# Finer score tables, more gathers and expert units beside the last attention, and a third of the tail's products on GpSimd

## The chip, the cores and the metric

The kernel runs on one NeuronCore of one Trainium2 chip, in one launch. The metric is the device time of that core in microseconds (us), the median of three runs. The engines are named as in the profile: PE (TensorE), DVE (VectorE), ACT (ScalarE), POOL (GpSimd) and SP (SyncE, which issues most DMAs).

## The reference, cut to what matters

A float32 tensor of 4 batch entries, 32 x 96 tokens and 256 channels goes through two layers. Layer 0 is a group norm and two state-space passes (along one axis, then the other). Layer 1 is an additive attention inside each batch entry, and then a graph network over all 12,288 tokens that decides how four expert networks are mixed:

```python
# attention, for each of 4 batch entries, 3072 tokens, U = 32
h = tanh(q[:, :, None, :] + k[:, None, :, :] + bh)      # q, k: 32 numbers a token
a = softmax(einsum('biju,u->bij', h, Wa) + ba)          # 3072 x 3072 scores
t = t + einsum('bij,bjd->bid', a, ln(t))

# graph: 1,048,576 edges, indices up to 65,536 (out-of-range ones clamp or are dropped)
h = (x_flat @ W_gat).reshape(M, HEADS, NUM_EXPERTS)     # 4 x 4 features a token
a_src, a_dst = (h * att_src).sum(-1), (h * att_dst).sum(-1)
e = leaky_relu(a_src[src] + a_dst[dst])
alpha = softmax of e over the edges into the same dst
agg = segment_sum(h[src] * alpha, dst)                  # 16 numbers a token
scores = layernorm(agg).reshape(M, HEADS, NUM_EXPERTS).mean(1)
w, idx = softmax(top_2(scores))
for ei in range(4):                                     # experts, 256 -> 512 -> 256
    hh = gelu(x @ W1[ei] + b1[ei])
    out += g[ei] * (hh @ W2[ei] + b2[ei])
```

The experts themselves don't need the graph; only their weights g do. The graph needs the features of every source and destination token, so it needs the attention's output.

## The kernel before, in words

The tokens lie in 96 tiles of 128 rows (24 tiles, `NT`, to a batch entry; 12, `T8`, to a half entry, of which there are 8, `N8`). The order of the work on PE, ACT, DVE and POOL is the order in which the Python program emits it: nothing is reordered, each engine runs its own list, and a wait holds everything behind it on that engine. What is interleaved, and how densely, is set by small budgets in microseconds that the program counts down while it is built. They are constants of the program, not measurements.

**The stages.** Until about 11.1 ms, Layer 0 and the attentions of entries 0 to 2 run together. Then the attention of entry 3 runs with other work beside it until 13.57 ms. A short drain follows, and then the tail: the graph and the rest of the experts.

**The last attention** (`Attention.units`). The attention goes in slots. Each has one tanh of 128 x 3072 on ACT (L1047), and eight matmuls of 384 columns on PE that turn an earlier tanh into scores (L1020, `scores`). Three tanh buffers lie between ACT and PE. After eight slots the 32 rows of one unit are complete: DVE takes the maximum (L1108), ACT the exponential (L1115), PE transposes (L1124) and multiplies with the values (L1133). After four units (32 slots) a tile is put together. For that POOL makes four small factors `sf` (L1192), on which PE waits (L1197). An entry has 768 slots and 96 units.

In each slot, `steps` in `whole` may add four kinds of work beside the attention:
- DVE sorts the edge list (`Edges.sort`) and, once it is sorted (`ed.listed`), makes one-hot tables of edges in bfloat16 (L1500), which PE multiplies into a count (`products`, L1514, eight matmuls, counted at 8 x `PRODUCT_US`).
- PE computes expert units ahead (`Experts.early`). A unit is 512 tokens through one expert: eight matmuls of 512 columns, sixteen of 256. Units go in pairs, and the two Gelus of a pair (L1965) come together on ACT.
- The two above draw on the same PE budget, `us_t`, which grows by `SLOT_US` a slot, less what the attention's own steps take. At most one set of products is taken in a slot; expert matmuls take what is left.
- POOL issues one or two gathers a slot (`columns`, L1276). A gather is an indirect DMA that fetches one row of a score table for each of 128 edges. `gather` reads destination scores from `tab_a`, `early` reads source rows from `tab_e`. The list `columns` has 360 of the first (half entries 0 to 5) and 216 of the second. It is begun when the tables of entries 0 to 2 are written. In each of these slots `pace` puts a copy of one element of the current tanh on POOL (L901), so that POOL can't run ahead of ACT.

`tab_a` is a DRAM tensor for each batch entry: a gather from one waits for all of its 24 tiles. The tables of entry 3 are written by `after` in four pieces while its attention still runs, the last of them behind it.

**The tail** (`tail`). A planner walks over half steps, six to an expert unit, with its own clock: 2.7 us a half step (`HALF_US`), 2.0 us more for each group of one-hot products (`GROUP_US`), 1.6 us for a gather that is still wanted (`GATHER_US`). What was gathered beside the attention is in `ed.have`, and only the rest is wanted. For each of 8 half entries there are five jobs of 12 edge columns. A job has scores, values, and three groups of four columns (`u0` = 0, 4, 8). For a group, `spread` makes on DVE a one-hot of lanes `ol`, a one-hot of tiles `oh` (L1663), and the product of `oh` with the features, `rh` (L1667, 128 x 960). A half step later `place` adds them up on PE in four matmuls of 240 columns (L1677). With all 120 groups planned, the expert units run on alone. When a quarter's groups are done, `finish` computes its gates on DVE, and then the kept expert outputs are weighted and summed there (L2006). The gathers of a half step come behind a `pace` of the tail: POOL copies a mark (L1612) that DVE writes (L1611), so POOL can't run ahead of DVE.

The lists `wanted`, `jobs` and `calls` are plain Python, so the interleaving of the tail follows from the counts alone.

Of the kernel before, what the change touches and what calls it, by code (L numbers as in the profile page):

```python
# [17 lines left out]
F32 = mybir.dt.float32  # L18
# [4 lines left out]
ALU = mybir.AluOpType  # L23
# [3 lines left out]
P = 128  # L27
B, NV, S, C = 4, 32, 96, 256
TOK = NV * S
M = B * TOK  # L30
NT = TOK // P
# [15 lines left out]
CT = 2  # L47
# [3 lines left out]
HEADS, NEXP, FF = 4, 4, 512  # L51
# [5 lines left out]
W1, W2, C1 = EW // 4, 512, 464  # L57
C2, CL, CY = 384, 112, 280
N8, T8, CE, LATE = 8, 12, 60, 24
EARLY = 4, 5, 0, 1, 6, 7  # L60
G1, K1 = 8, 4
GP, GG = 12, 4
EDGE_US = 2.3
# [1 line left out]
GATHER_US, HALF_US, GROUP_US, LAND_US = 1.6, 2.7, 2.0, 10.0  # L65
QUARTERS = 2, 0, 3, 1
KO_BUFS = 2
SLOT_US, PRODUCT_US = 1.2, 0.11
EU, EG = 32, 2
TB = 512  # L70
NQ, FC, NBLK_X = TB // P, FF // P, M // TB
# [2 lines left out]
ROW = HEADS + HF  # L74
# [777 lines left out]
class Attention:  # L852
# [4 lines left out]
    def __init__(self, ctx, tc, ident, a, x1, x2, xn2T, tab_s, tab_a, keys, l0):  # L857
        self.nc = nc = tc.nc
        self.ident, self.x1, self.x2, self.xn2T = ident, x1, x2, xn2T
        self.tab_s, self.tab_e, self.tab_a = *tab_s, tab_a  # L860
        pool = lambda name, bufs, **k: ctx.enter_context(
            tc.tile_pool(name=name, bufs=bufs, side="right", **k))
        const = self.const = pool("atc", 1)
        self.rows, self.th, self.wk = pool("atr", 2), pool("atb", TH_BUFS), pool("atw", 1)
        self.ps_e = pool("ate", PE_BUFS, space=PSUM)
        self.ps_v = pool("atv", PV_BUFS, space=PSUM)

        def load(name, shape, ap):
            t = const.tile(shape, F32, tag=name, name=name)
            nc.sync.dma_start(t, ap)  # L870
            return t

        self.l0, self.kq, self.krep, self.qsel = l0, keys, keys.krep, keys.qsel
        self.wa = load("wa_blk", [P, P // (4 * R_ATT), QU], a["wa_blk"])
        self.ba = load("ba_rep", [P, 1], a["ba_rep"])
        self.wg = load("wg", [P, KC, HF], a["W_gat"].rearrange("(k p) f -> p k f", p=P))
        self.asr = load("as_rep", [P, HF], a["as_rep"])
        self.adr = load("ad_rep", [P, HF], a["ad_rep"])
        self.eps = const.tile([P, 1], F32, tag="eps1", name="eps1")
        nc.vector.memset(self.eps, 1e-5)  # L880

        self.sel = const.tile([P, QU], F32, tag="sel", name="sel")
        nc.vector.tensor_tensor(self.sel, ident[:, :QU], ident[:, QU:2 * QU], ALU.add)
        for q in range(2, P // QU):
            nc.vector.tensor_tensor(self.sel, self.sel, ident[:, q * QU:(q + 1) * QU], ALU.add)
        self.state = [{} for _ in range(B)]

        self.extra, self.entry, self.col, self.asked, self.normed = 0.0, 0, 0, 0, 0
        self.now, self.reduces, self.more, self.tc = None, False, [], tc
        self.mark = const.tile([P, 1], F32, tag="mark", name="mark")  # L890

        self.later = []
# [318 lines left out]
    def after(self, b, t0=0, t1=NT):  # L1211

        nc, mv = self.nc, self.state[b]["mv2"]
        j0, N = t0 // CT, t1 // CT
        x2 = self.x2[b * TOK:(b + 1) * TOK, :]
        x = self.tiles_of(x2, j0)
        rs = self.inverse_roots(mv, t0, t1)
        yield
        for j in range(j0, N):
            rowsd = slice(b * TOK + j * CT * P, b * TOK + (j + 1) * CT * P)  # L1220
            ahead = self.tiles_of(x2, j + 1) if j + 1 < N else None
            for i in range(CT):
                self.normalized(x[:, i, :], x[:, i, :], mv, rs, j * CT + i)
            yield
            xT = self.transposed(x)
            nc.sync.dma_start(self.xn2T[:, :, rowsd].rearrange("k p m -> p k m"), xT)
            x = ahead
            yield
            ph = self.psum("ph")
            for i in range(CT):  # L1230
                for k in range(KC):
                    nc.tensor.matmul(ph[:, i * HF:(i + 1) * HF], xT[:, k, i * P:(i + 1) * P],
                                     self.wg[:, k, :], start=(k == 0), stop=(k == KC - 1))
            hb = self.wk.tile([P, CT, ROW], F32, tag="hb", name="hb")
            db = self.wk.tile([P, CT, HEADS], F32, tag="db", name="db")
            nc.vector.tensor_copy(hb[:, :, HEADS:],
                                  ph[:, :CT * HF].rearrange("p (n f) -> p n f", f=HF))
            tmp = self.wk.tile([P, CT, HF], F32, tag="gtmp", name="gtmp")
            for rep, dst in ((self.asr, hb), (self.adr, db)):
                nc.vector.tensor_tensor(tmp, hb[:, :, HEADS:],  # L1240
                                        rep.unsqueeze(1).to_broadcast([P, CT, HF]), ALU.mult)
                nc.vector.tensor_reduce(dst[:, :, 0:HEADS],
                                        tmp.rearrange("p n (h x) -> p n h x", x=NEXP),
                                        AX.X, ALU.add)
            n0 = b * NT + j * CT
            nc.sync.dma_start(self.tab_s[:, n0:n0 + CT, :], hb)
            if b < B - 1:
                nc.sync.dma_start(self.tab_e[:, n0:n0 + CT, :], hb)
            nc.sync.dma_start(self.tab_a[b][:, j * CT:(j + 1) * CT, :], db)
            if j == NT // CT - 1:  # L1250
                self.normed = b + 1
            yield


class Edges:
# [23 lines left out]

    def gather(self, k, c):  # L1280
        self.have.add((k, c, "d"))
        self.indirect(self.gd[:, k, c, :], self.tab_a[k // 2], self.di[:, k, c:c + 1])

    def early(self, k, c):
        self.have.add((k, c, "s"))
# [2 lines left out]
    def columns(self):  # L1288

        first = [(self.gather, k, c) for k in range(N8 - 2) for c in range(CE)]  # L1290
        return first + [(self.early, k, c) for k in EARLY for c in range(LATE, CE)]

    @staticmethod
    def halves(t):
# [58 lines left out]
    def sort(self):  # L1353


        nc, v, tc = self.nc, self.nc.vector, self.tc
        v.tensor_scalar(self.tiles, self.lanes[:, :NH], float(P), None, ALU.add)
        with ExitStack() as ctx:
# [4 lines left out]
            with tc.tile_pool(name="es", bufs=1) as lists:  # L1363
# [42 lines left out]
                c = w["keep"]  # L1406
# [10 lines left out]
                there, last = float((B - 1) * TOK + VALID), w["keep"][:, :C2]  # L1417
# [10 lines left out]
                part, tl = w["keep"][:, :W], w["keep"][:, W:2 * W]  # L1428
# [10 lines left out]
                n = N8 * CE  # L1439
# [11 lines left out]
                for of, rows in ((s3, self.si), (x3, self.di)):  # L1451
                    v.tensor_scalar(d, of, VALID - 1, None, ALU.bitwise_and)
                    v.tensor_scalar(lo, d, P - 1, None, ALU.bitwise_and)
                    v.tensor_scalar(hi, d, 7, None, ALU.logical_shift_right)
                    if rows is self.di:
                        v.tensor_scalar(lo, lo, float(NT), None, ALU.mult)
                        for q in range(1, B):
                            part = hi[:, 2 * q * CE:2 * (q + 1) * CE]
                            v.tensor_scalar(part, part, float(-q * NT), 0.0, ALU.add, ALU.max)
                    else:  # L1460
                        late, soon = split(lo)[:, :, :LATE], split(lo)[:, :, LATE:]
                        v.tensor_scalar(late, late, float(NH), None, ALU.mult)
                        v.tensor_scalar(soon, soon, float(NH - NT), None, ALU.mult)
                        tile = split(hi)[:, :, LATE:]
                        v.tensor_scalar(tile, tile, float(NH - NT - 1), None, ALU.min)
                    v.tensor_tensor(flat(rows), lo, hi, ALU.add)
                    yield 1.8
# [58 lines left out]
class Graph:  # L1526
# [35 lines left out]
    def tables(self):  # L1562
# [2 lines left out]
        self.hall = hall = new("hall", [P, NH, ROW])  # L1565
        adst = self.adst = new("adst", [P, NH, 2 * HEADS])
        nc.sync.dma_start(hall, self.tab_s)
        for q in range(4):
            nc.sync.dma_start(adst[:, q * NT:(q + 1) * NT, 0:HEADS], self.tab_a[q])
        last = self.last = new("last", [P, ROW])  # L1570
        nc.sync.dma_start(last, self.tab_s[P - 1, NH - 1, :].unsqueeze(0).to_broadcast([P, ROW]))

# [80 lines left out]
    def spread(self, k, g, u0):  # L1653
# [6 lines left out]
        for to, among, which in ((ol, ed.lanes, ed.lane),  # L1660
# [3 lines left out]
                                    which[:, k, cols].unsqueeze(2).to_broadcast([P, GG, n]),  # L1664
                                    ALU.is_equal)
        v = self.v[k, g][:, u0:u0 + GG, :]
        nc.vector.tensor_tensor(rh, oh.unsqueeze(3).to_broadcast([P, GG, T8, ROW]),  # L1667
                                v.unsqueeze(2).to_broadcast([P, GG, T8, ROW]), ALU.mult)
        return ol, rh

# [564 lines left out]
def whole(tc, a, dram, out):  # L2235
# [8 lines left out]

    tab_s = dram.tile([P, NH, ROW], F32, tag="tab_s", name="tab_s")
    tab_e = dram.tile([P, NH - NT, ROW], F32, tag="tab_e", name="tab_e")
    tab_a = [dram.tile([P, NT, HEADS], F32, tag=f"tab_a{b}", name=f"tab_a{b}") for b in range(B)]
    with ExitStack() as ctx:
        actx, lctx, ectx = ExitStack(), ExitStack(), ExitStack()
        with tc.manual_schedule(engines={E.PE, E.Activation, E.DVE, E.Pool}):  # L2250
# [8 lines left out]
            def steps():  # L2259
# [22 lines left out]
                while True:  # L2282
# [10 lines left out]
                    if columns:  # L2293
                        att.pace()
                        turn = 3 - turn
                        for f, k, c in columns[:turn]:
                            f(k, c)
                        del columns[:turn]
                    us_t = min(us_t, SLOT_US) + SLOT_US - att.extra
                    if ed.todo and us_t > 0:  # L2300
                        ed.todo.pop(0)()
                        us_t -= G1 * PRODUCT_US
# [108 lines left out]
```

## Time and profile before

| | us |
|---|---|
| median of 3 runs | 14503.21 (14501.98 to 14504.32) |
| the profiled execution | 14508.64 |
| its span, first to last instruction | 14506.8 |
| ACT busy | 12278.6 (85%) |
| PE busy | 11322.4 (78%) |
| DVE busy | 10473.8 (72%) |
| POOL busy | 9080.5 (63%) |

The busy shares are averages over stages that have different limits, so they say little by themselves. The two stages that the change touches are the last attention and the tail. Busy time of the four engines in five stretches, and the granted share of PE's clock:

| from, to (us) | what | PE | DVE | ACT | POOL | clock |
|---|---|---|---|---|---|---|
| 12100 to 13569 | last attention with gathers and products | 1312.8 of 1469 | 496.6 | 1436.2 | 690.5 | 0.97 |
| 13569 to 13640 | drain | 52.9 of 71 | 16.5 | 9.2 | 1.4 | 0.93 |
| 13640 to 13970 | tail, groups dense | 272.8 of 330 | 222.6 | 105.9 | 243.5 | 0.93 |
| 13970 to 14320 | tail, groups as gathers land | 300.8 of 350 | 250.6 | 86.4 | 232.3 | 0.94 |
| 14320 to 14507 | tail, expert units alone | 177.4 of 187 | 101.1 | 38.5 | 0.4 | 0.98 |

A busy PE is not a PE at its peak: matmuls are pipelined, and their ends are modelled. A gather's busy time on POOL is that of issuing it. The chain that ended last is empty in this profile, so the bounds have to be read from the stages and from the waits.

### The profile page before, as it was taken

The numbers are of one execution on the slowest core, as the hardware profiler recorded it, in microseconds if no ns is written. First come the engines' busy times: TensorE is split into PE (matmuls) and PEld (weight loads), VectorE is DVE, ScalarE is ACT, GpSimd is POOL, SyncE is SP. The second block draws the span as 40 slices with busy tenths as digits, with TensorE's granted clock in tenths as the row PEclk, the third lists the DMA queues.
The fourth block names the chain that finished last, engine by engine and source line by source line (L and its number), as shares of the span: only waits on it lengthen the run. The fifth ranks groups of instructions, "written<-read, shape, count | busy, mean of one in ns | idle before, by whom it ended". The sixth has DMA issues, their size and how long they took to land.

```text
span 14506.8 us, 224766 instructions
## 1 busy us (share of the span) xinstructions
PE 11322.4 (78%) x86704; PEld 5143.5 (35%) x86704; DVE 10473.8 (72%) x15217; ACT 12278.6 (85%) x9676; POOL 9080.5 (63%) x7108
## 2 busy tenths in 40 slices
PE   5777767777777777778887677788887788888888
PEld 2333322222232333333333233333333334443566
DVE  7888987787777877777777777757776785332376
ACT  4555569999999899999998899999999999999522
POOL 5777777777777667767776677747764003653373
PEclk8989978888888889989998899999989999999999
DMA  6778864445545444455554444435543100110233
GB/s 216 237 236 241 248 188 148 148 150 153 150 151 153 148 148 154 150 149 157 156 154 146 148 149 152 156 107 152 155 151 110 39 22 17 12 18 15 61 102 125
DMA packets 1199839, 1984.19 MB, mean 137 GB/s; under 512 B 418596, under 2 KB 646436, under 8 KB 1193636
## 3 DMA queue, kind: packets, MB, share of 16 engines
q1 hardware_dynamic: 1168036, 1963.77, 44.1%
q0 software_dynamic: 30720, 5.96, 0.9%
q8 instruction: 682, 11.17, 0.3%
q14 instruction: 401, 3.28, 0.1%
HBM read 1859.14 MB, written 110.18 MB: 136 GB/s over the span
## 4 chain that ended last, share of the span: by engine, by line


## 5 line engine op out<-in xcount | busy, mean ns | idle before, releaser
L1047 ACT ACTIVATE th<-krep,qsel 128x3072 f32<-128x3072 f32 x3072 | 8658.0, 2850 | 284.4 <-PE pe L1020 273.8
L1020 PE MATMUL pe<-th,wa_blk 128*32 128x384 f32 x49152 | 4933.7, 529 | 932.2 <-ACT pr L1115 691.0
L515 POOL TENSOR_TENSOR h<-h,bC 128x768 f32<-128x768 f32 x2048 | 3765.3, 1840 | 2769.4 <-DVE h L508 2198.2
L508 DVE TENSOR_TENSOR_SCAN h<-dA,dB 128x384 f32<-128x384 f32 x3008 | 2706.5, 941 | 895.9 <-ACT dA L470 673.8
L1020 PEld LDWEIGHTS pe<-th,wa_blk 128*32 128x32 f32 x49152 | 1468.5, 115 | 3408.8 <-issue 1877.1
L483 DVE TENSOR_TENSOR dB<-bB,dtu 128x768 f32<-128x768 f32 x1912 | 1809.9, 947 | 97.0 <-DMA bB<-bc 45.9
L522 POOL TENSOR_TENSOR h<-h 128x768 f32<-128x768 f32 x752 | 1413.5, 1880 | 53.6
L1133 PE MATMUL pv<-xn,pT 128*32 128x257 f32 x18432 | 1156.6, 401 | 216.7 <-DVE pT L1126 215.4
L470 ACT ACTIVATE dA<-dt,t_A 128x380 f32<-128x380 f32 x2048 | 1121.2, 571 | 230.2 <-DVE h L508 162.6
L534 PE MATMUL py<-h,ident 128*128 128x384 f32 x2176 | 930.0, 558 | 478.5 <-POOL h L515 370.4
L470 ACT ACTIVATE dA<-dt,d_A 128x372 f32<-128x372 f32 x2048 | 1107.2, 564 | 139.3 <-DVE h L508 91.8
L503 DVE TENSOR_TENSOR_SCAN h<-dA,dB 128x768 f32<-128x768 f32 x544 | 947.7, 1751 | 127.3 <-ACT dA L470 81.3
L1192 POOL TENSOR_SCALAR sf<-sel,f 128x32 f32<-128x32 f32 x384 | 137.3, 384 | 1239.3 <-ACT f L1188 1238.8
L1133 PEld LDWEIGHTS pv<-xn,pT 128*32 128x32 f32 x18432 | 598.4, 115 | 851.1 <-DVE pT L1126 373.7
L1108 DVE TENSOR_REDUCE nb<-pe 128x1 f32<-128x768 f32 x384 | 364.2, 948 | 729.0 <-PE pe L1020 697.1
L523 POOL TENSOR_TENSOR h<-h 128x384 f32<-128x384 f32 x752 | 790.4, 1051 | 59.0
L524 POOL TENSOR_TENSOR y<-y,h 128x384 f32<-128x384 f32 x752 | 777.1, 1033 | 59.0
L534 PEld LDWEIGHTS py<-h,ident 128*128 128x128 f32 x2176 | 420.2, 209 | 941.0 <-POOL h L515 583.5
L1124 PE MATMUL ptw<-ident,pr 128*128 128x128 f32 x2304 | 459.2, 314 | 306.4 <-DVE pT L1126 128.1
L1126 DVE COPY pT<-ptw 128x512 f32<-128x512 f32 (+1 forms) x768 | 417.6, 544 | 327.3 <-PE ptw L1124 315.4
L1276 POOL DMA_INDIRECT gd<-tab_a,di x480 | 498.3, 1038 | 159.2 <-issue 156.7
L1124 PEld LDWEIGHTS ptw<-ident,pr 128*128 128x128 f32 x2304 | 295.7, 159 | 770.9 <-issue 281.3
(329 smaller groups left out, 15071.9 us busy)
## 6 DMA issues: line engine op xcount, KB each, us to landing
bB<-bc SPq DMA_DIRECT2D x2048, 384.0 KB
bC<-bc SPq DMA_DIRECT2D x2048, 384.0 KB
x<-x SPq DMA_DIRECT2D x321, 128.0 KB
all<-kept SPq DMA_DIRECT2D x40, 1024.0 KB
kept<-ko SPq DMA_DIRECT2D x43, 512.0 KB
xt<-xn2T SPq DMA_DIRECT2D x41, 512.0 KB
qsel<-xn2T SPq DMA_DIRECT2D x75, 256.0 KB
kept<-eo SPq DMA_DIRECT2D x150, 128.0 KB
```

Source lines behind the costliest of these rows:

```text
L470: nc.scalar.activation(inner(dA[:, s * T:(s + 1) * T] if alone else self.dA[s][:, :T]), inner(blk["dt"][:, e, :]), AF.Exp, scale=blk["w"][ ...
L483: nc.vector.tensor_tensor(dB, blk["bB"].pop(j), z["dtu"].unsqueeze(1).to_broadcast([P, SB, T]), ALU.mult)
L503: nc.vector.tensor_tensor_scan(flat(h), dA[:, :SB * T], flat(dB), 0.0, ALU.mult, ALU.add)
L508: nc.vector.tensor_tensor_scan(h[:, s, :], self.dA[s][:, :T], dB[:, s, :], 0.0, ALU.mult, ALU.add)
L515: nc.gpsimd.tensor_tensor(h, h, blk["bC"].pop(j), ALU.mult)
L522: nc.gpsimd.tensor_tensor(h0, h0, h1, ALU.add)
L523: nc.gpsimd.tensor_tensor(h0[:, 0, :], h0[:, 0, :], h0[:, 1, :], ALU.add)
L524: nc.gpsimd.tensor_tensor(y[e], y[e], h0[:, 0, :], ALU.add)
L534: nc.tensor.matmul(z["py"], self.ident, h[:, s, :], start=(i == 0), stop=(i == DS - 1))
L1020: nc.tensor.matmul(pe[q * QU:(q + 1) * QU, j, :KQ // 2], self.wa[:, k, :], th[:, c0:c0 + KQ // 2], start=(k == 0), stop=(k == NK - 1))
L1047: nc.scalar.activation(th, s["krep"], AF.Tanh, bias=s["qsel"][:, col:col + 1])
L1133: nc.tensor.matmul(pv[q * QU:(q + 1) * QU, :C + 1], pT[:, i, q * QU:(q + 1) * QU], s["xn"][:, q * NK + i, :], start=(i == 0), stop=(i == N ...
```

## The change

Four edits go together.

1. `tab_a` becomes eight tensors of half an entry. A gather of the first half of entry 3 waits only for that half.
2. 96 more gathers are issued beside the last attention: 36 source columns of half entry 2 (`EARLY` has a seventh member), and the 60 destination columns of half entry 6, the first half of entry 3. Those may go once 12 tiles of entry 3 are written (`att.tiles`), and stand behind three quarters of the source columns; until then the next column that may go is taken.
3. The PE budget of a slot is 1.45 instead of 1.2 once the edge list is sorted. In the program that is built, 29 expert units instead of 22 are then computed ahead, and 30 instead of 37 are left to the tail.
4. In the tail, the third group of each job (`u0` = 8, 40 of 120) has its `rh` product made on POOL instead of DVE.

```diff
-EARLY = 4, 5, 0, 1, 6, 7
+EARLY = 4, 5, 0, 1, 6, 7, 2
-SLOT_US, PRODUCT_US = 1.2, 0.11
+SLOT_US, PRODUCT_US = (1.2, 1.45), 0.11
...
+            k, n = divmod(n0, T8)
+            nc.sync.dma_start(self.tab_a[k][:, n:n + CT, :], db)
+            self.tiles = b * NT + (j + 1) * CT
...
     def columns(self):
         first = [(self.gather, k, c) for k in range(N8 - 2) for c in range(CE)]
-        return first + [(self.early, k, c) for k in EARLY for c in range(LATE, CE)]
+        early = [(self.early, k, c) for k in EARLY for c in range(LATE, CE)]
+        own = [(self.gather, N8 - 2, c) for c in range(CE)]
+        n = len(early) * 3 // 4
+        return first + early[:n] + own + early[n:]
...
-        for q in range(4):
-            nc.sync.dma_start(adst[:, q * NT:(q + 1) * NT, 0:HEADS], self.tab_a[q])
+        for k in range(N8):
+            nc.sync.dma_start(adst[:, k * T8:(k + 1) * T8, 0:HEADS], self.tab_a[k])
...
-        nc.vector.tensor_tensor(rh, oh.unsqueeze(3).to_broadcast([P, GG, T8, ROW]),
+        to = nc.gpsimd if u0 == GP - GG else nc.vector
+        to.tensor_tensor(rh, oh.unsqueeze(3).to_broadcast([P, GG, T8, ROW]),
                                 v.unsqueeze(2).to_broadcast([P, GG, T8, ROW]), ALU.mult)
...
-                        for f, k, c in columns[:turn]:
-                            f(k, c)
-                        del columns[:turn]
-                    us_t = min(us_t, SLOT_US) + SLOT_US - att.extra
+                        for _ in range(turn):
+                            there = att.tiles >= B * NT - NT // 2
+                            n = next((n for n, (f, k, _) in enumerate(columns)
+                                      if there or k < N8 - 2 or f == ed.early), None)
+                            if n is not None:
+                                f, k, c = columns.pop(n)
+                                f(k, c)
+                    us_t = min(us_t, SLOT_US[0]) + SLOT_US[ed.listed] - att.extra
```

The rest of the diff makes the indices of the destination rows relative to a half entry instead of an entry (seven small operations on DVE in the sort instead of three).

More of the change, by code (lines that the diff above doesn't have):

```diff
@@ L888, in __init__ @@
         self.extra, self.entry, self.col, self.asked, self.normed = 0.0, 0, 0, 0, 0
-        self.now, self.reduces, self.more, self.tc = None, False, [], tc
+        self.now, self.reduces, self.more, self.tc, self.tiles = None, False, [], tc, 0
         self.mark = const.tile([P, 1], F32, tag="mark", name="mark")
@@ L1248, in after @@
                 nc.sync.dma_start(self.tab_e[:, n0:n0 + CT, :], hb)
-            nc.sync.dma_start(self.tab_a[b][:, j * CT:(j + 1) * CT, :], db)
+            k, n = divmod(n0, T8)
+            nc.sync.dma_start(self.tab_a[k][:, n:n + CT, :], db)
+            self.tiles = b * NT + (j + 1) * CT
             if j == NT // CT - 1:
@@ L1281, in gather @@
         self.have.add((k, c, "d"))
-        self.indirect(self.gd[:, k, c, :], self.tab_a[k // 2], self.di[:, k, c:c + 1])
+        self.indirect(self.gd[:, k, c, :], self.tab_a[k], self.di[:, k, c:c + 1])
     def early(self, k, c):
@@ L1455, in sort @@
                     if rows is self.di:
[L1456 to L1459, printed above, removed]
+                        v.tensor_scalar(lo, lo, float(T8), None, ALU.mult)
+                        for k in range(1, N8):
+                            part = hi[:, k * CE:(k + 1) * CE]
+                            v.tensor_scalar(part, part, float(-k * T8), 0.0, ALU.add, ALU.max)
                     else:
@@ L2246, in whole @@
     tab_e = dram.tile([P, NH - NT, ROW], F32, tag="tab_e", name="tab_e")
-    tab_a = [dram.tile([P, NT, HEADS], F32, tag=f"tab_a{b}", name=f"tab_a{b}") for b in range(B)]
+    tab_a = [dram.tile([P, T8, HEADS], F32, tag=f"tab_a{k}", name=f"tab_a{k}") for k in range(N8)]
     with ExitStack() as ctx:
```

## The prediction

> **What bounds the kernel now.** I read the table of busy time by stretch first: the page's shares average over stages with different limits. Columns: stretch, its length, then busy us of PE, weight loads, DVE, ACT and POOL, granted PE clock, DMA.
>
> ```profile
> 12100.00:13569.00 1469.00, 1312.79 (x13746) 611.92 (x13745) 496.59 (x966) 1436.23 (x591) 690.53 (x1020) 0.97 0.09 16
> 13640.00:13970.00 330.00, 272.78 (x1043) 204.93 (x1041) 222.57 (x556) 105.91 (x128) 243.46 (x253) 0.93 0.23 51
> 13970.00:14320.00 350.00, 300.84 (x1077) 215.35 (x1078) 250.61 (x625) 86.44 (x109) 232.25 (x275) 0.94 0.53 154
> 14320.00:14507.00 187.00, 177.42 (x629) 119.44 (x627) 101.09 (x225) 38.50 (x54) 0.38 (x1) 0.98 0.32 111
> ```
>
> Beside the last attention ACT is busy 1436 of 1469 us, PE 1313: ACT bounds, and PE has 156 us left. The last stretch is PE's alone. Next, ACT's groups in the first stretch, and the waits (from 12120 to 13560):
>
> ```profile
> L1047 ACT ACTIVATE th<-krep,qsel 128x3072 f32<-128x3072 f32 x490 | 1358.6, 2852 | 33.6 <-PE pe L1020 32.9 <-POOL mark L901 0.3 <-issue 0.3
> L1965 ACT ACTIVATE h<-h 128x2048 f32<-128x2048 f32 x10 | 18.7, 1904 | 0.3 <-DVE h L1960 0.2
> L1965 ACT ACT_TABLE_LOAD x5 | 6.4, 1283 | 0.1
> ...
> PE ptw L1124 <- ACT pr L1115: 43.7, 30, 8.5
> PE pe L1020 <- ACT th L1047: 40.7, 68, 4.9
> PE po L1197 <- POOL sf L1192: 25.8, 12, 3.6
> PE ph L1921 <- DVE h L1960: 14.2, 12, 1.9
> ```
>
> The tanh waits 33 us in 490 slots, nearly all for PE. Of PE's 156 idle us only 41 are waits for a tanh, which is true slack. The others are latencies (exponential, POOL's factors, DVE's evacuations).
>
> For the tail I read POOL's groups (13640 to 14320), and POOL's waits from 13655 to 13930, where the groups are dense:
>
> ```profile
> L1276 POOL DMA_INDIRECT gs<-tab_s,si x192 | 214.8, 1118 | 48.7 <-issue 48.6 <-DVE e L1638 0.2
> L1276 POOL DMA_INDIRECT gd<-tab_a,di x120 | 134.3, 1119 | 30.8 <-issue 30.8
> L1612 POOL COPY seen<-mark 1x1 f32<-1x1 f32 x143 | 50.1, 350 | 130.9 <-DVE mark L1611 128.1 <-issue 2.0
> ...
> POOL seen L1612 <- DVE mark L1611: 6.8, 4, 4.4
> ```
>
> A POOL at 70% busy looks free; it isn't. A gap of about 0.25 us ("issue") follows each gather, and in those 275 us POOL waited 6.8 us for a mark. It issued 170 gathers there: 275 / 170 = 1.62 us for one with gap and mark copy. POOL's queue is full in the dense part, and 384 gathers x 1.62 = 622 of the 647 us in which it gathers (13643 to 14290). PE, at 273 of 330, is close behind.
>
> **The change, part by part.** Sums are made against the profiled execution (14508.6 us, 1.8 above its span). It lies 5.4 us above the median.
>
> *Beside the attention, ACT.* In the built program's order 27 Gelus stand before the last tanh, in 14 pairs or singles, where 18 in 9 stood. That is 9 x 1.904 = 17.1 us, and 5 x 2 table loads (Gelu, then tanh again) x 1.283 = 12.8: 30 us on the engine that bounds. Nothing hides them.
>
> *Beside the attention, PE.* 57 more expert matmuls of 512 columns and 120 of 256 come between the first tanh and the last. Start to start at full clock the timeline has one of the first at 1.06 us, four of the second at 1.92: 60.4 + 57.6 = 118 us. ACT then needs 1466 us, PE 1431 busy us plus whatever latencies stay, in a stretch of 1469. The bounds: 0 beyond ACT's 30 if PE's wait for exponentials vanishes as PE falls behind (a late PE finds them ready), and 118 - 41 = 77 us if no wait but that for the tanh shrinks. I take 30, below the middle, as eight-slot stretches with four of the 256-column sets run at ACT's pace already. Behind a late PE stand scores, so tanh buffers, so ACT. Together +60, from +30 to +107.
>
> *Gathers beside the attention.* 96 gathers and 64 more mark copies go into POOL's queue past the factors `sf`: POOL has 778 us idle in the stretch, so their 96 x 1.3 and 64 x 0.23 us are covered. Where a tile's factors queue behind two gathers, PE waits up to 2.6 us, in up to six more tiles: 0 to 16 us, inside the range above. The new gathers from half entry 6 have no wait that lasts: they stand some 180 columns behind the point from which they may go. Without that cover they would cost 125 us of POOL, as they do in the tail. The eight table loads (four issues more, 0.35 us each on SP), 28 more DVE evacuations of 0.74 us and the index arithmetic lie under idle engines: 0; uncovered, some 25 us.
>
> *Drain.* Between the last tanh and the tail 16 expert matmuls of 256 columns fewer: -8 us (0 to -13 with the two Gelus that leave it).
>
> *Tail, what leaves.* Seven units: in the last stretch one Gelu set follows another at 13.8 us, so 7 x 13.8 = 97 us of PE. And 96 gathers, 96 x 1.62 = 155 us of POOL. Of DVE 40 `rh` products, 46 us.
>
> *Tail, what comes.* 40 products on POOL. No row shows one of 960 elements; the nearest do:
>
> ```profile
> L522 POOL TENSOR_TENSOR h<-h 128x768 f32<-128x768 f32 x752 | 1413.5, 1880 | 53.6
> L523 POOL TENSOR_TENSOR h<-h 128x384 f32<-128x384 f32 x752 | 790.4, 1051 | 59.0
> L1667 DVE TENSOR_TENSOR rh<-oh,v 128x960 f32<-128x960 f32 x120 | 139.1, 1159 | 4.1
> L561 DVE TENSOR_TENSOR dtu<-dt,xc x188: 539/882/2206, 1978.5 to 11061.0; 128x384 f32<-128x384 f32 x188
> ```
>
> 384 elements more cost 0.83 us, so 960 cost 1.88 + 0.41 = 2.3 us, against 1.16 on DVE. The broadcast operands could make it dearer; I bound it by 1.9 and 3.5 and take 2.3, next to L522. So POOL has 288 x 1.62 + 40 x 2.3 = 559 us of queue where it had 622: of the 155 us that the gathers free, 92 are given back.
>
> Two engines now meet. The last row above (fewest, median and most ns) is a DVE product with both inputs in SBUF, in the stage where POOL multiplies all the time: 0.54 us when free, 1.05 in the mean. L483, one of whose inputs is kept in PSUM, holds 0.915 to 0.957 us through the same stage. So a POOL product delays such a DVE instruction by some 0.5 us, and nearly all of DVE's work in the tail has both inputs in SBUF. I put 40 x 0.5 = 20 us on the graph's path (0 to 40). The Trainium skill, "SBUF — State Buffer", section "Who interferes with whom", says this in general: a DVE instruction with two SBUF inputs and a GpSimd instruction that reads SBUF exclude each other, and the second waits out the whole of the first. By it the 40 products would block DVE for up to 40 x 2.3 = 92 us, twice what they take off it; with that in the place of my 20 the tail's sum below would be +61 us at worst.
>
> *Tail, the sum.* Counted through the planner's loop, the graph ends at half step 149 before and 93 after, so 24.8 and 15.5 units are interleaved with it and 12.2 and 14.5 run behind it. The graph's part follows POOL: 622 to 559, and +20 for the collisions, so -43; the rest +2.3 x 13.8 = +32. Tail: -11. If PE bounded instead, -97. If the products on POOL, which now stand behind gathers and ahead of PE's `place`, add one more bubble of 1 us each: +29. Who waits: PE's `place`, behind it the units, behind them DVE for free one-hot buffers, behind that the mark on which POOL's next gathers wait.
>
> Sum: +60 - 8 - 11 = +41 us on 14508.6, 14549.6; on the median's scale, 5.4 lower, 14544.
>
> **The rivals.**
>
> *Both hide, a draw.* PE absorbs its 118 us in latencies, so only ACT's 30 remain; the drain gives 8; POOL's products don't collide, so the tail gives -63 + 32 = -31: -9 us, 14494. For it: single eight-slot stretches with as much on PE run at ACT's pace now. Against it: after the change nearly every one is like that, and there is nothing between them to catch up in.
>
> *Faster: the tail is PE's, not POOL's.* POOL's 1.62 us are then partly POOL keeping step with DVE's marks, and shrink when DVE has 46 us less to do. The tail falls with PE's seven units: +30 - 8 - 97 = -75 us, 14428. For it: PE at 273 of 330 us, and units among dense groups in which PE never pauses. Against it: 6.8 us of waits for marks. It decides once a gather with its gap costs under some 1.3 us, since 288 x 1.3 + 92 = 466 us is then near what PE needs for 15.5 units and 480 `place` matmuls.
>
> *Slower still.* PE misses its slack in full (+107) and the products add their bubble (+29): with the drain's -8, +128, 14631.
>
> *The change doesn't do what it says*: excluded by the built order, which holds 96 more gathers before the last tanh, 40 products on POOL and 30 units in the tail.
>
> **How the numbers follow.** What a measurement here can tell from no change is about 0.2%, 29 us. The forecast (+41, a loss) has 0.36, the heavier loss 0.10, the draw 0.30, the PE-bound tail 0.24. So slower 0.46, same 0.30, faster 0.24. The range, 14430 to 14625, leaves out the outer half of the PE-bound case and of the heavier loss, 0.17 in all; the forecast's own range, by its bounds, is 14495 to 14600.
>
> **What would show it.** Right: the last tanh ends 40 to 80 us later; ACT's tanh waits over 50 us for PE there; POOL's queue is full until the last gather, and PE waits for `rh` from POOL; units behind the graph still 13.8 us apart. Wrong: the attention ends no later than 30 us after its time before, or PE in the dense tail is over 90% busy with few waits for POOL, or a POOL product takes under 1.9 or over 3.5 us.

## The result, and the profile after

The changed kernel took 14571.9 us in the median (14561.4 to 14574.3, five runs) against 14502.0 beside it on the same chip: 1.0046 of before, 95% interval [1.0035, 1.0057], slower by more than the 0.2% that a measurement can tell. The forecast was 14544 in a range of 14430 to 14625. The profiled execution took 14562.8 us with a span of 14560.9, 54 us above that of before. The sign and the size are near the forecast; what stands behind them is not quite what it said.

By stage, from the trace: the first tanh of the last attention starts 9 us earlier than before (over the 14 executions of this document it spreads by 21 us, so this is no effect of the change that can be told); from its start to that of the last tanh 2397 us, where it was 2350 (+47); from there to the tail's first Gelu 79, was 94 (-15); from there to the end 882, was 852 (+31). The last is the surprise: seven units of work have left the tail, and it is longer. Stretches of the changed kernel, columns as before (length; busy us of PE, weight loads, DVE, ACT, POOL; granted PE clock; DMA): the end of the attention, the tail up to the last `place`, the tail behind it.

```profile
12100.00:13608.00 1508.00, 1395.54 (x14021) 672.31 (x14021) 521.72 (x1001) 1462.14 (x607) 796.04 (x1178) 0.98 0.12 22
13679.00:14328.00 649.00, 463.36 (x1657) 350.25 (x1656) 418.73 (x967) 160.48 (x194) 402.22 (x414) 0.85 0.25 70
14328.00:14561.00 233.00, 212.27 (x740) 140.32 (x738) 146.55 (x323) 44.45 (x63) 0.38 (x1) 0.99 0.49 163
```

In the first row ACT is at 97% and PE at 93%: the attention is still ACT's. In the second no engine is near its limit: PE 71%, DVE 65%, POOL 62%. PE idles there for 649 - 463 = 186 us. The changed kernel's ACT groups in the attention (12100 to 13608) and its waits (12120 to 13608; total, times, longest):

```profile
L1971 ACT ACTIVATE h<-h 128x2048 f32<-128x2048 f32 x17 | 31.6, 1904 | 0.1
L1971 ACT ACT_TABLE_LOAD x9 | 11.5, 1283 | 0.2
...
ACT th L1047 <- PE pe L1020: 33.0, 41, 1.5
PE ptw L1124 <- ACT pr L1115: 25.5, 12, 7.5
PE pe L1020 <- ACT th L1047: 17.8, 11, 5.3
PE po L1197 <- POOL sf L1192: 13.5, 8, 3.5
```

Against the same rows of before the Gelus and table loads have grown, and PE's waits have shrunk: for the exponential from 43.7 to 25.5 us, for a tanh from 40.7 to 17.8, for POOL's factors from 25.8 to 13.5, although more gathers stand in POOL's queue. The late PE found its inputs ready. In the tail, the waits beside the graph (13679 to 14328) and POOL's groups (13640 to 14330):

```profile
DVE ol L1668 <- PE pa L1683: 124.0, 47, 20.2
POOL seen L1617 <- DVE mark L1616: 111.9, 22, 18.0
PE pa L1683 <- POOL rh L1673: 106.9, 23, 18.3
PE pa L1683 <- DVE rh L1673: 76.0, 14, 13.3
...
L1278 POOL DMA_INDIRECT gs<-tab_s,si x192 | 204.8, 1066 | 52.0 <-issue 49.7 <-PE pa L1683 0.9 <-DVE ko L1999 0.3
L1673 POOL TENSOR_TENSOR rh<-oh,v 128x960 f32<-128x960 f32 x40 | 74.0, 1851 | 46.7 <-DVE oh L1668 19.8 <-DVE mark L1616 16.4 <-issue 7.0
```

PE waits for POOL, DVE for PE (a free one-hot buffer), POOL for DVE (a mark): a circle in which each engine waits for the next, with nobody's queue full. A product on POOL takes 1.85 us, not 2.3. A few lines of the timeline (start, duration, engine, line) show a second thing:

```profile
13844.08 0.20 DVE L1668 TENSOR_TENSOR oh<-tiles,tile 128x48 f32<-128x48 f32 x1
13844.21 0.35 DVE L1653 TENSOR_TENSOR v<-eg,v 128x192 f32<-128x192 f32 x1
13844.45 1.81 POOL L1673 TENSOR_TENSOR rh<-oh,v 128x960 f32<-128x960 f32 x1 [1.39 <-DVE mark L1616]
13844.48 1.85 DVE L1643 TENSOR_TENSOR e<-eg,gd 128x48 f32<-128x48 f32 x1
```

`e<-eg,gd` has 48 elements, and takes 0.2 us when it is alone. It came 0.03 us behind POOL's product and ended with it. So there were two candidates for the tail's loss, the wait (below the wait theory) and the exclusion of DVE by POOL's products (the lock theory), and a third, that the change's other parts had made the tail worse (the density theory).

### The profile page after: what moved, and what is told of

It is laid out like the page before. It is cut to its first block, busy times and chain, and to the rows that moved or that the text cites. A ratio compares the mean times of both kernels' runs of the same rounds, so it can differ in the third digit from the quotient of the medians.

```text
span 14560.9 us, 224891 instructions
## 1 busy us (share of the span) xinstructions
PE 11339.7 (78%) x86704; PEld 5152.2 (35%) x86704; DVE 10489.6 (72%) x15152; ACT 12278.4 (84%) x9658; POOL 9108.4 (63%) x7155
## 4 chain that ended last, share of the span: by engine, by line
ACT 38%; PE 24%; DVE 18%; issue 6%; POOL 5%; DMA 2%; SPq 1%; DVEq 0%; POOLq 0%; ACTq 0%
ACT th L1047 27%; PE pe L1020 10%; ACT dA L470 6%; PE pv L1133 4%; DVE h L508 4%; DVE dB L483 2%; POOL h L515 2%; PE po L1935 2%; DVE h L503 1%; PE ph L1927 1%; ACT pr L1115 1%; PE pz L585 1%; PE pc L1519 1%; DVE y L2012 1%; PE ptw L1124 1%
## 5 line engine op out<-in xcount | busy, mean ns | idle before, releaser
L522 POOL TENSOR_TENSOR h<-h 128x768 f32<-128x768 f32 x752 | 1412.7, 1879 | 53.6
```

What stands on the lines that cost most here:

```text
L522: nc.gpsimd.tensor_tensor(h0, h0, h1, ALU.add)
```

## The experiments

Each run has its own kernel before beside it; ratios are to that. Attention is from the start of the first tanh to that of the last, tail is first Gelu of the tail to the end, graph is the part of it up to the last `place`, and PE idle is the graph's length less PE's busy time there, all from the profiled execution, in us. The attention's four executions with before's units in it spread over 2331 to 2350, the eight with seven units more over 2383 to 2400.

| run | ratio, 95% | attention | tail | graph | PE idle |
|---|---|---|---|---|---|
| before | 1 | 2350 | 852 | 666 | 98 |
| after | 1.0046 [1.0035, 1.0057] | 2397 | 882 | 649 | 186 |
| e1 all on DVE | 0.9974 [0.9965, 0.9983] | 2383 | 765 | 528 | 96 |
| e2 product only | 1.0107 [1.0091, 1.0122] | 2331 | 989 | 803 | 197 |
| e3 shadow product | 1.0041 [1.0027, 1.0055] | 2388 | 854 | 617 | 160 |
| e4 ring of four | 0.9997 [0.9988, 1.0006] | 2384 | 793 | 566 | 120 |
| e5 blind product | 1.0019 [1.0010, 1.0028] | 2383 | 828 | 595 | 144 |
| e6 blind iota | 0.9983 [0.9974, 0.9992] | 2386 | 776 | 540 | 102 |
| e7 slot back | 1.0005 [0.9996, 1.0014] | 2336 | 853 | 517 | 90 |
| e8 ring, all on DVE | 0.9945 [0.9931, 0.9958] | 2387 | 718 | 490 | 64 |
| e9 ring alone | 0.9974 [0.9964, 0.9984] | 2341 | 818 | 634 | 71 |
| e10 ring, no gathers | 0.9962 [0.9949, 0.9976] | 2400 | 746 | 646 | 87 |
| e11 ring, slot 1.6 | 0.9921 [0.9908, 0.9935] | 2445 | 649 | 474 | 50 |
| e12 no Gelu beside | 0.9929 [0.9915, 0.9942] | 2319 | 769 | 535 | 100 |

**Everything but the product.** The changed kernel with

```diff
-        to = nc.gpsimd if u0 == GP - GG else nc.vector
+        to = nc.vector
```

> The changed kernel with the third product of each half entry back on DVE; the gathers and the Gelus beside the attention stay. All three theories give the attention and the drain as after (last tanh about 38 us later than before, drain 15 us shorter). Wait theory (the product on POOL stands behind gathers and ahead of PE's place; the loop through the two one-hot buffers costs the time): PE's waits for POOL's rh (107 us) go, its waits for DVE's rh grow from 166 to some 200 us, and the tail falls from 882 to 800-840 us: 14480 to 14520 us in all. Lock theory (POOL's product shuts DVE out): the tail loses 40 x 1.8 = 73 us of exclusion and gets 46 us of products, about 855 us: 14535. Density theory (parts that shorten the graph, not the product, cost the tail): the tail stays at 870-890 us: 14550-14575.

It is faster than before by 0.26%, more than any theory allowed: the tail is 117 us shorter than after. So the other three parts were a gain, and the product alone turned it into a loss: 117 us of tail by the profiles, 0.72% or 104 us by the runs. The density theory is out.

**The product alone.** The kernel before with only
```diff
+        to = nc.gpsimd if u0 == GP - GG else nc.vector
-        nc.vector.tensor_tensor(rh, oh.unsqueeze(3).to_broadcast([P, GG, T8, ROW]),
+        to.tensor_tensor(rh, oh.unsqueeze(3).to_broadcast([P, GG, T8, ROW]),
```

> The kernel before with nothing but the third product on POOL: same gathers, same units beside the attention. Wait theory: the attention is unchanged; PE waits some 100 us for POOL's rh, as POOL's queue of 384 gathers is longer here, and the tail grows from 852 to 890-930 us: 14540 to 14580 us in all. Lock theory: between +0 and +27 us (73 of exclusion less 46 of products): 14500 to 14530. Density theory: POOL has 40 x 1.8 = 73 us more to do and no idle time if its queue was full: +30 to +70 us, by POOL's busy share, with few waits of PE for POOL's rh.

The tail grew by 137 us, more than the wait theory's 40 to 80 and far more than the lock theory's 27. PE waited 133.7 us for POOL's `rh`, and POOL 139.9 us for DVE's marks: POOL's throughput is not the limit.

**The load without the wait.** DVE makes all products, and POOL makes the third one again for nobody:

```diff
+        if u0 == GP - GG:
+            r2 = self.wl[:, :GG * T8, :].rearrange("p (u n) f -> p u n f", u=GG)
+            nc.gpsimd.tensor_tensor(r2, oh.unsqueeze(3).to_broadcast([P, GG, T8, ROW]),
+                                    v.unsqueeze(2).to_broadcast([P, GG, T8, ROW]), ALU.mult)
```

> The changed kernel with all products on DVE as in the run with all on DVE, and the third one made once more on POOL, into a tile that nobody reads (the part of wl that is done with). POOL has the same work in the same place in its queue, and takes DVE's port as often, but PE waits for DVE's product alone. Wait theory: within 20 us of the run with all on DVE (some 40 x 0.5 us of collisions at most), 14490 to 14535 us. Lock theory: as slow as the changed kernel or slower, since DVE has 46 us more to do: 14570 to 14620. The DVE instruction e<-eg,gd (0.2 us alone) and the one-hot products show by their mean how often they are shut out.

PE no longer waits for POOL, and 90 of the 117 us are still lost. The wait theory as I had put it, that PE's wait is the main cost, falls. The run has a flaw, though: DVE may not overwrite `oh` until POOL has read it (48 us of waits). So the next pair took the data away as well.

**Four sets of buffers.** The third and fourth set of `ol`, `oh`, `rh` lie in the room of `hall` and `wl`, and a place comes a half step later:

```diff
+        self.turn = not self.turn
+        if deep and self.turn:
+            big, m, n = self.big(), GG * T8 * ROW, GG * P
+            rh = big[:, :m].rearrange("p (u n f) -> p u n f", u=GG, n=T8)
...
-                    at(half + 1, lambda k=k, g=g, u0=u0, ends=ends:
+                    at(half + 1 + deep, lambda k=k, g=g, u0=u0, ends=ends:
```

> The changed kernel with the product on POOL, but four sets of one-hot buffers instead of two (two of them in the room of the own-edge tables, free by then) and every place one half step (some 7 us) later. Attention and drain as after. Wait theory: POOL's product has 7 us more before PE wants it, so PE's waits for POOL's rh fall from 107 us to under 30 and those for DVE's rh too; the tail falls from 882 to 800-840 us: 14480 to 14520 us in all. Lock theory: DVE is shut out as before, PE waits for DVE instead, the tail stays over 865 us: 14545 to 14575. Density theory: no change, 14560 to 14575.

The tail fell by 89 us, into the range of the wait theory, but not by the wait that it named. In the profile of this run (13666 to 14231; `big` is the room of the added sets):

```profile
PE pa L1694 <- POOL big L1684: 74.4, 17, 9.5
PE pa L1694 <- POOL rh L1684: 31.5, 8, 18.7
DVE ol L1679 <- PE pa L1694: 22.1, 2, 18.7
POOL seen L1621 <- DVE mark L1620: 18.3, 10, 5.3
```

PE still waited 106 us for POOL's products, as in the changed kernel (106.9), where under 30 were expected. What fell were the other waits of the circle: PE's for DVE's products (76.0 to some 14), DVE's for a free buffer (124.0 to 22.1), POOL's for marks (111.9 to 18.3). And later runs, without products on POOL, show that the ring covers any delay of a group, not this one alone.

**The load without anybody's data, and the load without reads.** In the place of the shadow product either of

```diff
+            nc.gpsimd.tensor_tensor(flat(self.wl), flat(self.hall), flat(self.hall), ALU.mult)
...
+            nc.gpsimd.iota(self.wl[:].rearrange("p n f -> p (n f)")[:, :n].bitcast(I32), [[1, n]],
+                           base=0, channel_multiplier=0)
```

> As the run with the shadow product (all real products on DVE), but the 40 extra products on POOL multiply hall by itself into the part of wl that is done with: 960 elements, both inputs in SBUF, but nobody's data, so no one-hot buffer is held and neither DVE nor PE waits for it. It stands at the same place in POOL's queue. The run with all on DVE was at 0.9974 of before, the shadow product at 1.0041. Queue theory (1.8 us of POOL ahead of the gathers cost that much, 40 x some 2.15 with its gap): the tail is 70 to 90 us longer than the 765 us with all on DVE, ratio 1.002 to 1.004. Lock theory (POOL's reads shut DVE's two-input instructions out): +40 to +75 us in the tail, ratio 1.000 to 1.003, and the same load without reads costs nothing. Loop theory (what cost the shadow product is that DVE waits until POOL has read the one-hots, 48 us, and then POOL for DVE): under +25 us, ratio below 0.9992.

> As the blind product, but POOL's 40 extra instructions are iotas of 1680 elements into wl, which write SBUF and read nothing; by the iota of 464 elements, 0.52 us, one takes 1.8 to 1.9 us. Queue theory: as much as the blind product, tail +70 to +90 us against all on DVE. Lock theory: under +20 us in the tail, whatever the blind product costs, ratio about 0.998. Loop theory: under +25 us, like the blind product.

Here the theories part. First three lines of the blind product: its POOL group, its whole tail by engine, and DVE's weighted sums (fewest, median and most ns); then the same of the iota:

```profile
L1676 POOL TENSOR_TENSOR wl<-hall 128x960 f32<-128x960 f32 x40 | 73.8, 1844 | 8.3 <-issue 7.6
13668.00:14495.00 827.00, 662.67 (x2395) 481.54 (x2393) 621.14 (x1329) 205.08 (x257) 450.20 (x415) 0.91 0.34 101
L2014 DVE SCALAR_TENSOR_TENSOR y<-all,gates,y x320: 472/485/2507, 13897.4 to 14406.7; 128x256 f32<-128x256 f32 x160
```

```profile
L1676 POOL IOTA wl<- 128x1680 int32 x40 | 61.8, 1545 | 7.2 <-issue 6.8
13671.00:14447.00 776.00, 652.34 (x2397) 475.11 (x2395) 565.08 (x1329) 205.41 (x257) 421.94 (x416) 0.93 0.36 107
L2015 DVE SCALAR_TENSOR_TENSOR y<-all,gates,y x320: 470/485/534, 13888.1 to 14358.5; 128x256 f32<-128x256 f32 x160
```

And the whole tail with all on DVE:

```profile
13686.00:14451.00 765.00, 648.63 (x2396) 473.12 (x2394) 561.30 (x1329) 205.13 (x257) 370.23 (x375) 0.93 0.37 109
```

DVE does the same 1329 instructions in all three. With 62 us of writing on POOL its busy time is 4 us longer and the tail 11; with 74 us of reading and writing 60 us longer, and the tail 63. A sum that takes 0.485 us takes up to 2.5. What POOL's products cost by themselves is not POOL's time: it is DVE's, shut out while POOL reads SBUF. The lock theory holds, and the queue theory (that POOL's time ahead of the gathers is the cost) has at most 11 us of the 63. (The iota is 0.3 us shorter than the product; in proportion that would be 13.)

So the tail can be followed step by step: 765 us with all on DVE, 776 when POOL only writes, 828 when it reads nobody's data, 854 when it reads `oh`, which DVE must then keep, and 882 when PE waits for POOL's product itself, although DVE then has 46 us less to do.

**The units that move.** The run with all on DVE, with

```diff
-SLOT_US, PRODUCT_US = (1.2, 1.45), 0.11
+SLOT_US, PRODUCT_US = (1.2, 1.2), 0.11
```

> The run with all on DVE with SLOT_US at (1.2, 1.2): more gathers beside the attention, but units there as in the kernel before. It prices the seven units that move. If they cost the attention 47 us (30 of Gelus and table loads, 17 of PE stalls), as the two profiles say, and the drain 8 to 15 us less, against seven units of 13.8 us to 21 us each in the tail, then this run has an attention of 2350 us and a tail 97 to 150 us longer than 765: slower than the run with all on DVE by 60 to 110 us, ratio 1.0015 to 1.005. If the units behind the graph are free in the tail because they fill PE's waits for rh, it is 20 us faster to 20 us slower: ratio 0.996 to 0.999.

The seven units cost the attention 47 us and bring the tail 88, less than the 97 to 150 expected, so the ratio fell between the two classes: moving them gains 0.31%. The run shows something more important. It differs from the kernel before in its gathers alone (96 fewer in the tail), and its tail is as long as before's. The graph part of before, then graph part and rest of this run:

```profile
13655.00:14321.00 666.00, 568.46 (x2107) 417.66 (x2106) 471.60 (x1175) 192.35 (x236) 471.46 (x522) 0.94 0.38 103
```

```profile
13628.00:14145.00 517.00, 427.27 (x1658) 325.95 (x1657) 395.53 (x965) 160.28 (x194) 367.94 (x374) 0.92 0.29 72
14145.00:14480.00 335.00, 313.11 (x1075) 207.40 (x1073) 174.94 (x378) 63.70 (x91) 0.38 (x1) 0.97 0.39 132
```

The graph ends 149 us sooner, and the units that no longer run beside it run behind it. PE idles 98 us beside the graph in the one and 90 in the other. The tail's length is PE's work, plus some 95 us that PE waits for 120 groups, with 384 gathers as with 288.

**Where the 95 us are.** The diff of the ring on the run with all products on DVE, and on the kernel before:

> The run with four sets of one-hot buffers and the places one half step later, with all products on DVE. With the product on POOL the ring brought the tail from 882 to 793 us, with two sets and the product on DVE it is 765 us. If ring and product save the same waits (PE's for rh, DVE's for free buffers), the tail is 740 to 765 us and the ratio 0.995 to 0.9975. If POOL's and DVE's times add up (PE waited 117 us for DVE's rh with all on DVE, 15 with the ring), the tail falls by up to 90 us, to 680 us: ratio 0.991 to 0.993.

> The kernel before with nothing changed but the four sets of one-hot buffers and the places one half step later. The ring took 47 us off the tail of the run with all on DVE (765 to 718), PE's idle time beside the graph from 96 to 64. PE theory of the tail (its length is PE's work plus what PE waits for the groups; gathers don't set it): PE idles 98 us beside the graph here too, so the tail falls by 30 to 55 us, ratio 0.9962 to 0.998. Queue theory of the tail (384 gathers at 1.62 us set when the graph ends): the ring changes nothing for POOL, ratio 0.9993 to 1.0007.

PE's idle time falls to 64 and 71 us and the tails by 47 (between the two ranges expected) and 34 us: these were waits of PE for `rh` and of DVE for a free buffer, in the kernel before as well. The second is outside "queue theory", inside "PE theory". With the ring the product on POOL costs 793 - 718 = 75 us instead of 117, so some 42 of the 117 were the circle of waits. These 42 rest on single profiles: by the runs the product costs 0.72% without the ring and 0.52% with it, a difference of 29 us, give or take some 31 by their intervals.

**Gathers, and more units, under the ring.** The first is the kernel before with SLOT_US (1.2, 1.45) and the ring, the second the ring with all on DVE and
```diff
-SLOT_US, PRODUCT_US = (1.2, 1.45), 0.11
+SLOT_US, PRODUCT_US = (1.2, 1.6), 0.11
```

> The run with the ring and all on DVE without its first part: the kernel before with SLOT_US at (1.2, 1.45) and the ring, so 30 units in the tail but 384 gathers in it instead of 288. PE theory of the tail: the 96 gathers are worth little, as setting SLOT_US back showed (96 gathers fewer, tail 853 against 852 us); ratio 0.994 to 0.9965, tail 720 to 745 us. Queue theory: with fewer units to interleave, 96 gathers of 1.4 to 1.6 us now stick out: tail 800 us or more, ratio 0.999 or above.

> The run with the ring and all on DVE with SLOT_US at (1.2, 1.6): four more units leave the tail (26 instead of 30). The seven before cost the attention 47 us and took 88 off the tail. If four more do it at the same rate, 24 us are won: ratio 0.992 to 0.9935. If PE has no latencies left to fill beside the attention, each costs there 14 us or more and the draw or a loss follows: ratio 0.9945 to 0.997.

The 96 gathers are worth 27 us of tail when 30 units are left to cover them, and nothing when there are 37 (e7, without the ring): here 646 of the 746 us are graph, and only 5 units are left behind it. The two ratios overlap, so the 27 us rest on the profiles. The second run, e11, is the best version found, 0.9921 of before: 14382.9 us against 14496.1 beside it; its interval still touches that of e8. Four units more cost the attention 58 us, 15 each where the first seven cost 7, as the second class expected; as if PE had no more latencies there to fill (not tested apart). But they took 69 us off the tail, 17 each, and so the ratio is in the first class.

**ACT's share of the attention.** The run with all on DVE without

```diff
-            for h in hs:
-                nc.scalar.activation(h, h, AF.Gelu)
```

> The run with all on DVE without the Gelus of the units beside the last attention (left out of the computation; PE's, DVE's and DMA's work on those units stays). It prices ACT's share of what the units cost the attention: 27 Gelus of 1.9 us and 14 x 2 table loads of 1.28 us, 87 us. If ACT alone bounds there, the attention falls from 2383 us by 75 to 90 us and the drain by up to 10: ratio 0.991 to 0.992. If PE is the bound as soon as ACT has less to do (1363 us busy of 1469 beside its latencies), it falls by 30 to 60 us: ratio 0.993 to 0.9955. Under 30 us: the stalls of PE were what the seven units cost, not their Gelus.

The attention falls by 64 us of the 87 that the Gelus and their table loads were counted at (ACT is busy 2296.5 us in it in e1 and 2212.8 here, 84 less): between the two classes. ACT's time counts there for about three quarters; the rest, PE takes.

## Why the prediction was right, and where not

**Attention, +60.** Measured +47 (+49 between the means of the executions with and without the units). ACT's 30 us were called certain; by e12's 64 of 87 they are worth some 22, and PE's stalls the other 25 (worked out, not measured apart). The lower bound's reason, that a late PE finds its exponentials ready, is what the waits show. The stalls did not come as tanh waits for PE of over 50 us, as I had named: that row went from 25.7 (12120 to 13560) to 33.0. The last tanh ended 38 us later, just short of the 40 to 80 named.

**Gathers beside the attention, 0.** Right: PE's wait for `sf` fell, and the attention is no shorter without them (2400 us in e10, 2387 in e8). **Drain, -8.** Measured -15 (-10 in e1).

**Tail, what leaves.** This is the step that failed. "POOL's queue is full in the dense part" was read from 1.62 us per gather with few waits for marks, and the graph's part was made to follow POOL. But POOL was keeping step with a chain of groups: without the 96 gathers nothing of the tail went (e7). The trace of before had a sign of it that the prediction didn't use, POOL's wait from 13930 to 14300:

```profile
POOL seen L1612 <- DVE mark L1611: 60.9, 12, 13.5
```

The price of the dense part didn't hold there: 622 us of queue and these 60.9 of waiting are more than the 647 us in which POOL gathered. In the changed kernel the queue wasn't full either (111.9 us of waits for marks). What left it was the seven units, 88 us where the rival "the tail is PE's" said 97. For the first three parts that rival was right: e1 is faster than before.

**Tail, the product.** I put 92 us of POOL's queue and 20 of collisions on it, 112, and 117 were measured (e1 to after). The size is right by accident, and so the forecast's tail is near for reasons other than its own. The 92 are at most 13 (e6). A product took 1.85 us and not 2.3, below the bound of 1.9 that I had named as a sign of error: I had priced it in proportion to its elements, while 960 of them cost what 768 cost in L522 (1.88). The 20 were some 50 to 60: DVE's busy time rose by 60 us with the same instructions in e5, and in the tail of the changed kernel it is 565 us (419 + 147 in the rows above) where e1 has 561, though 40 products, 46 us, have left it. And the bubble of 1 us a product, which I left to the heavier case, was there: the circle of waits is worth some 42 us, by the ring. How these parts add up to 117 is shown only by the steps from 765 to 882 above.

So the sum, remade: +47 in the attention, -10 in the drain (e1), -87 in the tail for parts one to three (852 to 765), +117 for the product: +67, against +0.46%, 67 us, in the runs and +54 in the profiles, where the first tanh came 9 us earlier and the drain was -15. My tail of -11 was -123 (POOL) +112; it was -87 +117.

**The rule.** The Trainium skill, "SBUF — State Buffer", section "Who interferes with whom", said that the second of two such instructions waits out the whole of the first. The timeline rows and e5 against e6 agree: the write-only iota, which the same section exempts, cost DVE 4 us, the reading product 60. By the rule the tail's sum was +61 "at worst", by mine -11; +31 was measured, between the two. I had taken 0.5 us a collision from L561's mean, 1.05 against 0.54 us. That mean holds the free cases too. In the tail most products meet such an instruction, and it is held for nearly a whole product. Counted in the traces, 28 DVE instructions of the changed kernel's tail took over 0.3 us more than the median of their kind in e1, 48 us in all, each of them across one of the 40 products; 35 in e5 (61 us), 3 in e6 (2.5 us), none in e1.

**Behind the graph** the units stood 13.8 us apart as said, except some at 16 to 20 us, where kept sums crowd DVE.

## What to carry to other kernels

An engine that shows little waiting and no gaps may still be keeping step with a loop: to learn whether its queue bounds a stage, take some of its work away and see whether the stage ends sooner, before pricing a change by it. An offload from DVE to GpSimd is priced by what DVE loses while GpSimd reads SBUF, not by GpSimd's idle time: here 46 us of products moved and some 50 to 60 us of exclusion came back, before any wait. Where several engines pass small groups in a circle through two buffers, more depth was worth more (34 to 89 us) than moving work between the engines.

## What the hardware showed that was not expected

A DVE instruction with two SBUF inputs could be held for longer than a usual product of POOL lasts: `e<-eg,gd`, 0.2 us when free, took up to 2.41 us beside products of 1.82 us in the median (first row, of the changed kernel), and 0.24 at most without them (second, all on DVE).

```profile
L1643 DVE TENSOR_TENSOR e<-eg,gd x21: 196/208/2414, 13700.0 to 14187.1; 128x48 f32<-128x48 f32 x21
```

```profile
L1643 DVE TENSOR_TENSOR e<-eg,gd x21: 196/201/243, 13707.4 to 14092.3; 128x48 f32<-128x48 f32 x21
```

By the timeline the longest of them started 0.52 us ahead of the product and ended with it:

```profile
13911.79 2.41 DVE L1643 TENSOR_TENSOR e<-eg,gd 128x48 f32<-128x48 f32 x1
13912.31 1.82 POOL L1673 TENSOR_TENSOR rh<-oh,v 128x960 f32<-128x960 f32 x1
```

Seven of the 28 held instructions began 0.28 to 0.57 us before their product. So by the recorded starts the first of the two can be the one that is held, which the rule above doesn't say; as POOL's spans are rough, it stays open whether that is the true order.

The tail's matmuls are the same in e1 and after, yet PE is busy 649 us in the one and 676 in the other (463 + 212 us in the rows after, 2397 matmuls). The granted clock beside the graph was 0.92 with PE 82% busy, and 0.85 with PE 71% busy. So about 27 of the 117 us appear as slower matmuls. That idling lowers the clock was not tested apart; before (0.94 at 85%) and the run with the product only (0.88 at 75%) stand in the same order.
